# An expert's hidden features formed turned: weights standing in TensorE's array, and a ScalarE copy of each tile's weights

## The chip, the cores and the metric

The kernel runs on one core of a Trainium2 chip. A time is the device time of one execution in microseconds (us). Before the change it was 764.09 us, the median of three runs (763.78 to 767.37). One more execution was profiled: it took 762.74 us, and its span, from the first instruction to the last, is 761.0 us. All rows, durations and starts below are those of this one execution. Engines are named as the profile names them: PE is TensorE's matmul and PEld its weight load, DVE is VectorE, ACT is ScalarE, POOL is GpSimd, SP is SyncE; a name with a q (SPq, ACTq) is that engine's own queue of DMA issues and register work. L1168 is line 1168 of the kernel.

## What is computed

4 x 1024 tokens of 256 features pass through cross-attention (16 heads, a context of 77 rows) with a residual and layer norms, and then through a mixture of 32 experts with a shared expert beside it. Everything is float32. The part that the change touches is the expert:

```python
def swiglu(x, w1, w2, w3):
    return jax.nn.silu(x @ w1) * (x @ w3) @ w2
...
scores = jax.nn.softmax(xf @ Wg, axis=-1)
weights, indices = jax.lax.top_k(scores, 4)
for e in range(32):
    tok, w = ...                      # the tokens that chose expert e, and their gates
    out = swiglu(xf[tok], W1[e], W2[e], W3[e]) * w[:, None]
    y = y.at[tok].add(out)
z = swiglu(xf, Ws1, Ws2, Ws3)         # the shared expert, all tokens
return y + z
```

W1[e] and W3[e] are 256 x 128 and W2[e] is 128 x 256. An expert's tokens are worked in tiles of 128 rows.

## The kernel before

**Stages.** Up to about 400 us the kernel does the attention, 32 tiles of 128 queries, and for each block of 512 tokens the routing: the normalised rows are scattered to DRAM (`xr`), sorted by expert. From 449 us to 720 us it works the experts' tiles; this is the stage of the change. From 721 us to the end it does the shared expert's last three blocks, gathers the experts' results and stores.

**Experts' tiles.** At least 128 tiles are worked in a loop written out in full; after it a `Switch` chooses, by a number found at run time, how many more groups of eight tiles follow (here two, so 144 tiles in all). All experts' weights lie in SBUF in one tile `we`; for each expert there are W1 and W3, cut in two halves of 128 input features (`KC` = 2), and then W2. Which expert a tile belongs to is known only at run time: its number is loaded into a register (`registers`, L1084, a TENSOR_LOAD for eight tiles at a time), and an instruction's address is computed from it.

Four steps make a tile, and the loop runs them as a pipeline: in iteration j, step i is done for tile j - i, so PE's order in an iteration is in(j), mid(j-1), turn(j-2), out(j-3).

- `expert_in` (L1160, L1162): PE turns the tile's 128 gathered rows (two transposes, `pgT`), DVE copies them to `gT`.
- `expert_mid` (L1168, L1176, L1177): PE multiplies with `gT` standing in the array and 256 columns of W1 and W3 moving, for both halves (`peh`: tokens down, features across). ACT applies silu to the first 128 columns, DVE multiplies by the other 128: `h`.
- `expert_turn` (L1182, L1184): PE turns `h` (`phT`), ACT copies it to `ehT`.
- `expert_out` (L1192, L1196, L1197): PE multiplies `ehT` by W2 (`py`), ACT scales by the token's gate into `y`, POOL scatters `y` to DRAM (`ys`) with an indirect DMA.

A float32 matmul shows in the profile as two records, each a weight load and a pass of the moving columns; a transpose shows as one.

**Beside the tiles.** SP fetches the rows of eight tiles at a time (`fetch`, L1106, once in eight iterations, seven ahead), reads back results that are complete (`take`, L1220), and loads blocks of the shared expert's input (`fetch_shared`, L577, into three rotating buffers `sx`; the sixth block on ACT's queue, behind the drained loop). DVE finds each group's places (`find`, L1122 to L1153) and, from tile 88 on, adds the results taken (L1234, L1236). Two blocks of the shared expert (L589, L600, L606, L617, L632) are put between the tiles: block 1 at iterations 3 to 7, block 2 where the loop drains and the Switch ends.

**What sets the order.** Inside `as_written()` every engine runs its instructions in the order in which they are written; nothing is moved by a scheduler. PSUM is one ring of eight banks. Tiles in SBUF have as many buffers as their pool says (`bp`: two, where not stated otherwise), and an instruction that writes a buffer waits for the readers of what was there. Code that follows the Switch waits for each engine's work inside it where it touches the same buffers.

Of the kernel before, what the change touches and what calls it, by code (L numbers as in the profile page):

```python
# [16 lines left out]
P = 128  # L17
NE = 32
# [12 lines left out]
def kernel(  # L31
# [65 lines left out]
    def bank(name):  # L97
        return ps.tile([P, 512], F32, tag="bank", name=name)
# [979 lines left out]
        sends(3)  # L1078
        shared_add(z)
    late_stack.close()  # L1080
    sxp = ctx.enter_context(tc.tile_pool(name="sxp", bufs=3, side="right"))

    def registers(table, j0, engine, most):
        _, vals = nc.values_load_multi_w_load_instructions(  # L1084
            table[0:1, j0 : j0 + RG],
            engines=[engine],
            min_val=0,
            max_val=most,
            skip_runtime_bounds_check_because="whole numbers by their making",
        )  # L1090
        return vals
# [1 line left out]

    bp_stack = ExitStack()
    bp = bp_stack.enter_context(tc.tile_pool(name="bp", bufs=2, reuse_waits="tile"))
    ev, groups = [], {}

    def table(j):
        return (*tabs["a"], j) if j < NA else (*tabs["z"], j - NA)
# [1 line left out]
    def fetch(j):  # L1101

        g = bp.tile([P, RG, ROW], F32, tag="g", name=f"g_{j}")
        r_tab, e_tab, _, _, jt = table(j)
        for i, r in enumerate(registers(r_tab, jt, mybir.EngineType.SP, NE * PLACES)):
            got = nc.sync.dma_start(g[:, i, :], xr[ds(r, P), :])  # L1106
            for x in early if j < NA else scatters:
                tc.add_manual_dep(got.ins, x.name, SYNC, reason="reads what was scattered")
            if j < NA:
                tc.declare_no_dep(got.ins, group="lates", reason="distinct rows")  # L1110
                tc.add_to_no_dep_group("firsts", got.ins)
        ev.extend(registers(e_tab, jt, mybir.EngineType.PE, NE - 1))
        groups[j // RG] = [g]

    def find(j, step):
# [28 lines left out]
        else:  # L1144
# [8 lines left out]
                nc.vector.tensor_tensor(place_, n[3][:, :, 0], far, ALU.add)  # L1153
            n.append(place_)

    def expert_in(j, _):
        g = groups[j // RG][0]
        pt = bank(f"pgT_{j}")
        for k in range(KC):
            nc.tensor.transpose(pt[:, k * P : (k + 1) * P], g[:, j % RG, k * P : (k + 1) * P], ident)  # L1160
        gT = bp.tile([P, KC, P], F32, tag="gT", name=f"gT_{j}")
        nc.vector.tensor_copy(gT.rearrange("p k t -> p (k t)"), pt[:, :D])  # L1162
        return gT

    def expert_mid(j, gT):
        ph = bank(f"peh_{j}")
        for k in range(KC):
            nc.tensor.matmul(  # L1168
                ph[:, : 2 * H],
                gT[:, k, :],  # L1170
                we[:, ds(ev[j] * EW + k * 2 * H, 2 * H)],
                start=(k == 0),
                stop=(k == KC - 1),
            )
        h = bp.tile([P, H], F32, tag="h", name=f"h_{j}")
        nc.scalar.activation(h, ph[:, :H], AF.Silu)  # L1176
        nc.vector.tensor_tensor(h, ph[:, H : 2 * H], h, ALU.mult)  # L1177
        return h

    def expert_turn(j, h):  # L1180
        pt = bank(f"phT_{j}")
        nc.tensor.transpose(pt[:, :P], h, ident)  # L1182
        hT = bp.tile([P, P], F32, tag="ehT", name=f"ehT_{j}")
        nc.scalar.copy(hT, pt[:, :P])  # L1184
        return hT

    def expert_out(j, hT):
        if j in (NE_, NM_) and j not in upto:
            assert len(sents) == j
            upto[j] = list(sents)  # L1190
        py = bank(f"py_{j}")
        nc.tensor.matmul(py[:, :D], hT, we[:, ds(ev[j] * EW + KC * 2 * H, D)], start=True, stop=True)  # L1192
        y = bp.tile([P, D], F32, tag="y", name=f"y_{j}", bufs=6)
        own, place_ = groups[j // RG][3:]
        i = j % RG
        nc.scalar.activation(y, py[:, :D], AF.Identity, scale=own[:, i, 1:2])  # L1196
        sent = nc.gpsimd.indirect_dma_start(  # L1197
            out=ys,
            out_offset=bass.IndirectOffsetOnAxis(ap=place_[:, i : i + 1], axis=0),
            in_=y,  # L1200
            in_offset=None,
        )

        tc.declare_no_dep(sent.ins, group="results", reason="distinct places")
        tc.add_to_no_dep_group("results", sent.ins)
        for j0 in (NE_, NM_):
            if j >= j0:

                tc.declare_no_dep(sent.ins, group=f"takes {j0}", reason="distinct places")
                tc.add_to_no_dep_group(f"results {j0}", sent.ins)  # L1210
        sents.append(sent.ins)
# [34 lines left out]
            out[r0 : r0 + HC * P, :].rearrange("(c p) d -> p c d", p=P), y0[blk][:, c0 : c0 + HC, :]  # L1246
        )

    steps = [expert_in, expert_mid, expert_turn, expert_out]
    made = {}  # L1250
    BL = BM - 1
    adds, adds_l = (
# [2 lines left out]
    with as_written():  # L1255
        fetch(0)
        fetch_shared(1, nc.sync)
        for j in range(NM_ + len(steps)):
            if j % RG == 1 and j + RG - 1 <= NM_:
                fetch(j + RG - 1)  # L1260
            if j in (4 * RG + 4, 5 * RG + 4, 6 * RG + 4):
                fetch_shared(j // RG - 2, nc.sync)
            if j == NE_ + 3:
                for i in range(3):
                    take(i)
            for i, step in enumerate(steps):
                jj = j - i
                if 0 <= jj < NM_:
                    made[jj, i + 1] = step(jj, made.pop((jj, i), None))
            if j in (2, 5, 8, 11):  # L1270
                next(tz)

            for blk, j0 in ((1, 3), (2, NM_)):
                if j == j0:
                    shared_in(blk, 0, AF.Silu)
                    sends(3)
                if j == j0 + 1:
                    shared_mid(blk, 0)
                    shared_in(blk, 1, AF.Silu)
                    sends(3)  # L1280
                if j == j0 + 2:
                    shared_mid(blk, 1)
            if j == 6:
                shared_out(1)
                sends(2)
            assert not left or j < 6
            if j == 7:
                shared_add(1)
            if NE_ + 8 <= j < NM_:
                for i, step in adds[:1]:  # L1290
                    add_taken(i, step, BE * NC)

                    if step == TOPK // 2 and i % HC == 0 and HC <= i <= 2 * NC:
                        store(i // HC - 1, nc.sync)
                del adds[:1]
            if j < NM_ and j % RG in (0, 1, 2):
                find(j // RG * RG, j % RG)
            if j == NM_ - 2 * RG:
                more = {
                    e: nc.values_load(  # L1300
                        tabs["more"],
                        engines=[e],
                        min_val=0,
                        max_val=(NJ - NM_) // RG,
                        skip_runtime_bounds_check_because="at most as many tiles as are laid out",
                    )
                    for e in mybir.ALL_ENGINES
                }
                tc.switch_hint(more, (NJ - NM_) // RG + 1, label="more")
            if j == NM_ + 2:  # L1310
                fetch_shared(5, nc.scalar)
    assert not adds
    ahead = groups[NM_ // RG][0]
    for n in tc.Switch(more, (NJ - NM_) // RG + 1, hint="more"):
        end = NM_ + n * RG
        groups.clear(), made.clear()
        adds = list(adds_l)
        groups[NM_ // RG] = [ahead]
        del ev[NM_ + RG :]
        with as_written():  # L1320
            for i in range(3):
                take(BE * NC + i)
            for j in range(NM_, end + len(steps)):
                if j % RG == 1 and j + RG - 1 < end:
                    fetch(j + RG - 1)
                for i, step in enumerate(steps):
                    jj = j - i
                    if NM_ <= jj < end:
                        made[jj, i + 1] = step(jj, made.pop((jj, i), None))
                if j < end and j % RG in (0, 1, 2):  # L1330
                    find(j // RG * RG, j % RG)
                if j == end:
                    shared_out(2)
                if j == end + 1:
                    shared_add(2)
                if j >= NM_ + 6:
                    for i, step in adds[: 1 + j % 2]:
                        add_taken(i, step, BL * NC)
                    del adds[: 1 + j % 2]
            for i, step in adds:  # L1340
                add_taken(i, step, BL * NC)
# [26 lines left out]
    with as_written():  # L1368
        come = {hb: gather(hb) for hb in (12, 13, 14, 15, 10, 11)}
        shared_in(3, 0, AF.Silu)  # L1370
        shared_in(3, 1, AF.Silu)
        shared_mid(3, 0)
        store(4)
        shared_mid(3, 1)
# [80 lines left out]
```

## Time and profile before

| what | value | where in the profile |
|---|---|---|
| median of three runs | 764.09 us | runs |
| profiled execution, its span | 762.74 us, 761.0 us | runs, page's head |
| granted TensorE clock, mean | 0.989 | cores |
| PE busy, PEld busy | 95%, 71% of the span | page, part 1 |
| DVE, ACT, POOL busy | 63%, 53%, 53% | page, part 1 |
| experts' stage | 449.4 us (first `pgT`) to 720.1 us (last `py`) | tiles pgT, py |
| 450 to 724 us: PE busy | 263.1 of 274 us | windows |
| tiles, records of `pgT`, `peh`, `phT`, `py` on PE | 144; 288, 576, 144, 288 | tiles |

How to read it: "busy" joins the spans of instructions, which overlap on PE, so the cost of a PE instruction is not its duration but the distance from its start to the next one's. A row of groups names line, engine, operation, the tile written and the tiles read, the count, and durations. A row of waits says which engine stood idle at which line until which other line was done.

### The profile page before, as it was taken

The page shows a single profiled execution, that of the slowest core. Times are in us where ns is not written, and L with a number is a line of the kernel's source. Part 1 is how long each engine was busy: PE and PEld are TensorE (multiplying, and loading weights), DVE is VectorE, ACT ScalarE, POOL GpSimd, SP SyncE. Part 2 cuts the span into 40 slices and gives each one's busy share as a digit, 9 for nine tenths or more (in the row PEclk, how much of TensorE's full clock was granted, in tenths as well). Part 3 has the DMA queues.
Part 4 walks back from the last instruction along what each step waited for, and adds up shares of the span by engine and source line. Part 5 has one row for each costly group of instructions (what it writes and reads, how often), then busy time and mean ns, then how long its engine had stood idle before and what let it go on. Part 6 is the DMA issues. An engine that isn't in the chain of part 4 may idle for free. (4 is left out here: it accounts for less than half of the span.)

```text
span 761.0 us, 13078 instructions
## 1 busy us (share of the span) xinstructions
PE 720.0 (95%) x3515; PEld 536.6 (71%) x3515; DVE 478.2 (63%) x1368; ACT 402.3 (53%) x1730; POOL 404.1 (53%) x492
## 2 busy tenths in 40 slices
PE   7999999999999999999987779999999999999996
PEld 5866777677777767777763457788888887876754
DVE  2965565777877878776757433644545466645766
ACT  2658567666777576766553002455555555544310
POOL 1003343346777878777786655565565555553500
PEclk9999999999999999999998989999999999999999
DMA  8930000402217131513136451555746579847594
GB/s 284 342 113 1 1 1 1 132 7 87 100 59 253 47 127 52 170 59 120 74 97 210 140 189 65 159 173 183 224 161 195 166 262 311 258 127 244 186 342 163
DMA packets 78599, 111.98 MB, mean 147 GB/s; under 512 B 8949, under 2 KB 63667, under 8 KB 78515
## 3 DMA queue, kind: packets, MB, share of 16 engines
q1 hardware_dynamic: 60319, 68.76, 29.4%
q0 software_dynamic: 13056, 36.72, 13.0%
q10 hardware_dynamic: 5140, 5.55, 2.1%
q8 instruction: 32, 0.52, 0.3%
q14 instruction: 52, 0.43, 0.2%
HBM read 62.36 MB, written 48.64 MB: 146 GB/s over the span
## 5 line engine op out<-in xcount | busy, mean ns | idle before, releaser
L327 ACT ACTIVATE p<-sc,mx 128x77 f32<-128x77 f32 x512 | 159.5, 352 | 93.2 <-DVE mx L319 93.2
L1197 POOL DMA_INDIRECT ys<-y,place x144 | 138.9, 964 | 124.1 <-ACT y L1196 102.0
L1168 PE MATMUL peh<-we,gT 128*128 x576 | 150.7, 385 | 6.9 <-DVE gT L1162 5.4
L378 PE MATMUL po<-we,pT 128*128 128x256 f32 (+1 forms) x640 | 147.3, 383 | 4.8 <-DVE pT L365 3.4
L555 POOL DMA_INDIRECT xr<-xn,row x128 | 128.1, 1000 | 41.1 <-issue 33.1
L342 POOL TENSOR_TENSOR p<-p,su 128x385 f32<-128x385 f32 (+1 forms) x96 | 91.1, 974 | 97.5 <-DVE su L337 76.5
L311 PE MATMUL sc<-we,qT 128*128 128x385 f32 (+1 forms) x384 | 138.9, 509 | 0.9 <-POOL qT L297 0.9
L378 PEld LDWEIGHTS po<-we,pT 128*128 128x128 f32 (+1 forms) x640 | 118.4, 190 | 27.1 <-DVE pT L365 5.8
L327 ACT ACTIVATION_READ_ACCUMULATOR p<-sc,mx 128x1 f32 x512 | 119.3, 233 | 0.0
L1168 PEld LDWEIGHTS peh<-we,gT 128*128 128x128 f32 x576 | 99.2, 192 | 16.7 <-DVE gT L1162 6.5
L311 PEld LDWEIGHTS sc<-we,qT 128*128 128x128 f32 x384 | 71.1, 189 | 54.3 <-issue 27.7
L1176 ACT ACTIVATE h<-peh 128x128 f32<-128x128 f32 x144 | 40.0, 278 | 116.0 <-PE peh L1168 76.3
L1177 DVE TENSOR_TENSOR h<-peh,h 128x128 f32<-128x128 f32 x144 | 41.9, 291 | 87.1 <-ACT h L1176 80.2
L1192 PE MATMUL py<-we,ehT 128*128 x288 | 86.1, 381 | 0.0
L1196 ACT ACTIVATE y<-py,own 128x256 f32<-128x256 f32 x144 | 68.3, 475 | 17.8 <-PE py L1192 2.0
L319 DVE TENSOR_REDUCE mx<-sc 128x5 f32<-128x385 f32 (+1 forms) x96 | 54.3, 576 | 32.8 <-PE sc L311 30.1
L1162 DVE COPY gT<-pgT 128x256 f32<-128x256 f32 x144 | 60.5, 420 | 19.5 <-PE pgT L1160 9.1
L1160 PE MATMUL pgT<-ident,g 128*128 128x128 f32 x288 | 55.1, 274 | 1.3 <-DMA g<-xr 0.5
L1160 PEld LDWEIGHTS pgT<-ident,g 128*128 128x128 f32 x288 | 40.1, 142 | 17.2 <-issue 2.3
L1192 PEld LDWEIGHTS py<-we,ehT 128*128 128x128 f32 x288 | 43.6, 191 | 11.6 <-issue 0.8
L589 PE MATMUL ph<-sx,ws 128*128 128x512 f32 x96 | 46.0, 628 | 1.6 <-DVE y L1236 1.0
L360 PEld LDWEIGHTS pp<-ident,p 128*128 128x128 f32 x320 | 36.1, 139 | 11.4 <-issue 5.5
(227 smaller groups left out, 927.3 us busy)
## 6 DMA issues: line engine op xcount, KB each, us to landing
g<-xr SPq DMA_DIRECT2D x144, 136.0 KB
gx<-ys SPq DMA_DIRECT2D x20, 512.0 KB
gy<-ys SPq DMA_DIRECT2D x6, 1024.0 KB
xr<-y SPq DMA_DIRECT2D x1, 4352.0 KB
y<-in_x SPq DMA_DIRECT2D x8, 512.0 KB
xnd<-xnT SPq DMA_DIRECT2D x6, 512.0 KB
we<-in_W SPq DMA_DIRECT2D x8, 384.0 KB
out<-y ACTq DMA_DIRECT2D x12, 256.0 KB
```

Source lines behind the costliest of these rows:

```text
L311: nc.tensor.matmul(sc[:, : (h1 - h0) * SK], qTs[blk][:, k, o : o + P], mq[:, b, k, h0 * SK : h1 * SK], start=(k == 0), stop=(k == KC - 1),)
L319: nc.vector.tensor_reduce(mx[:, h0:h1], sv, AX.X, ALU.max, negate=True)
L327: nc.scalar.activation(probs[t][:, h, :], sv[:, h - h0, :], AF.Exp, bias=mx[:, h : h + 1], accum_out=su[:, h : h + 1],)
L342: nc.gpsimd.tensor_tensor(p[:, h0:h1, :], p[:, h0:h1, :], su[:, h0:h1].unsqueeze(2).to_broadcast([P, h1 - h0, SK]), ALU.mult,)
L378: nc.tensor.matmul(po[:, :D], pT[:n, i, :], vo[b][:n, i, :], start=(i == 0), stop=(i == KT - 1))
L555: sct = nc.gpsimd.indirect_dma_start(out=xr, out_offset=bass.IndirectOffsetOnAxis(ap=row[:, i : i + 1], axis=0), in_=xn[:, c, :], in_offse ...
L1160: nc.tensor.transpose(pt[:, k * P : (k + 1) * P], g[:, j % RG, k * P : (k + 1) * P], ident)
L1162: nc.vector.tensor_copy(gT.rearrange("p k t -> p (k t)"), pt[:, :D])
L1168: nc.tensor.matmul(ph[:, : 2 * H], gT[:, k, :], we[:, ds(ev[j] * EW + k * 2 * H, 2 * H)], start=(k == 0), stop=(k == KC - 1),)
L1192: nc.tensor.matmul(py[:, :D], hT, we[:, ds(ev[j] * EW + KC * 2 * H, D)], start=True, stop=True)
L1196: nc.scalar.activation(y, py[:, :D], AF.Identity, scale=own[:, i, 1:2])
L1197: sent = nc.gpsimd.indirect_dma_start(out=ys, out_offset=bass.IndirectOffsetOnAxis(ap=place_[:, i : i + 1], axis=0), in_=y, in_offset=None,)
```

## The change

- `expert_mid` now lets W1's and W3's four blocks of 128 x 128 stand in the array and `gT` (128 columns) move. The features come out down and the tokens across, so silu and product write `ehT` at once. `expert_turn` is gone: no `phT`, no copy of it; in its place stands `expert_rest`, which does nothing.
- Standing weights are read from a fixed address: ACT first copies the tile's 128 x 512 block of `we` to a buffer `w` (`weigh`, two buffers), at an address from its own registers (`eva`, loaded for ACT as `ev` is for PE).
- That copy is a pipeline step of its own, `expert_weigh`, so there are five steps: in(j), weigh(j-1), mid(j-2), rest(j-3), out(j-4). ACT's order in an iteration is w(j-1), silu(j-2), y(j-4).
- Buffers: `gT` three (two before), `ehT` three, `y` five (six), `sx` two (three). For that, the shared expert's fifth block is fetched on ACT's queue at the drained loop's end, and the sixth behind the tiles, after `shared_in(3, 1)`.
- `take` and the first adds are one iteration later.

```diff
-    sxp = ctx.enter_context(tc.tile_pool(name="sxp", bufs=3, side="right"))
+    sxp = ctx.enter_context(tc.tile_pool(name="sxp", bufs=2, side="right"))
...
         ev.extend(registers(e_tab, jt, mybir.EngineType.PE, NE - 1))
+        eva.extend(registers(e_tab, jt, mybir.EngineType.Activation, NE - 1))
...
+    def weigh(j):
+        fixed[j] = bp.tile([P, KC * 2 * H], F32, tag="w", name=f"w_{j}")
+        nc.scalar.copy(fixed[j], we[:, ds(eva[j] * EW, KC * 2 * H)])
...
-        gT = bp.tile([P, KC, P], F32, tag="gT", name=f"gT_{j}")
+        gT = bp.tile([P, KC, P], F32, tag="gT", name=f"gT_{j}", bufs=3)
...
     def expert_mid(j, gT):
+        w = fixed.pop(j)
         ph = bank(f"peh_{j}")
-        for k in range(KC):
-            nc.tensor.matmul(
-                ph[:, : 2 * H],
-                gT[:, k, :],
-                we[:, ds(ev[j] * EW + k * 2 * H, 2 * H)],
...
-        h = bp.tile([P, H], F32, tag="h", name=f"h_{j}")
-        nc.scalar.activation(h, ph[:, :H], AF.Silu)
-        nc.vector.tensor_tensor(h, ph[:, H : 2 * H], h, ALU.mult)
-        return h
-
-    def expert_turn(j, h):
-        pt = bank(f"phT_{j}")
-        nc.tensor.transpose(pt[:, :P], h, ident)
-        hT = bp.tile([P, P], F32, tag="ehT", name=f"ehT_{j}")
-        nc.scalar.copy(hT, pt[:, :P])
+        for f in range(2):
+            for k in range(KC):
+                nc.tensor.matmul(
+                    ph[:, f * P : (f + 1) * P],
+                    w[:, (2 * k + f) * H : (2 * k + f + 1) * H],
+                    gT[:, k, :],
...
+        hT = bp.tile([P, P], F32, tag="ehT", name=f"ehT_{j}", bufs=3)
+        nc.scalar.activation(hT, ph[:, :P], AF.Silu)
+        nc.vector.tensor_tensor(hT, ph[:, P : 2 * P], hT, ALU.mult)
+        return hT
+
+    def expert_weigh(j, gT):
+        weigh(j)
+        return gT
+
+    def expert_rest(j, hT):
         return hT
...
-        y = bp.tile([P, D], F32, tag="y", name=f"y_{j}", bufs=6)
+        y = bp.tile([P, D], F32, tag="y", name=f"y_{j}", bufs=5)
...
-    steps = [expert_in, expert_mid, expert_turn, expert_out]
+    steps = [expert_in, expert_weigh, expert_mid, expert_rest, expert_out]
...
-            if j in (4 * RG + 4, 5 * RG + 4, 6 * RG + 4):
+            if j in (4 * RG + 4, 5 * RG + 4):
                 fetch_shared(j // RG - 2, nc.sync)
-            if j == NE_ + 3:
+            if j == NE_ + 4:
...
-            if NE_ + 8 <= j < NM_:
+            if NE_ + 9 <= j <= NM_:
...
             if j == NM_ + 2:
-                fetch_shared(5, nc.scalar)
+                fetch_shared(4, nc.scalar)
...
         shared_in(3, 1, AF.Silu)
+        fetch_shared(5, nc.scalar)
         shared_mid(3, 0)
```

More of the change, by code (lines that the diff above doesn't have):

```diff
@@ L1095 @@
     bp = bp_stack.enter_context(tc.tile_pool(name="bp", bufs=2, reuse_waits="tile"))
-    ev, groups = [], {}
+    ev, eva, groups = [], [], {}
     def table(j):
@@ L1154, in find @@
             n.append(place_)
+    fixed = {}
+    def weigh(j):
+        fixed[j] = bp.tile([P, KC * 2 * H], F32, tag="w", name=f"w_{j}")
+        nc.scalar.copy(fixed[j], we[:, ds(eva[j] * EW, KC * 2 * H)])
     def expert_in(j, _):
@@ L1165, in expert_mid @@
     def expert_mid(j, gT):
+        w = fixed.pop(j)
         ph = bank(f"peh_{j}")
-        for k in range(KC):
-            nc.tensor.matmul(
-                ph[:, : 2 * H],
-                gT[:, k, :],
-                we[:, ds(ev[j] * EW + k * 2 * H, 2 * H)],
-                start=(k == 0),
-                stop=(k == KC - 1),
-            )
-        h = bp.tile([P, H], F32, tag="h", name=f"h_{j}")
-        nc.scalar.activation(h, ph[:, :H], AF.Silu)
-        nc.vector.tensor_tensor(h, ph[:, H : 2 * H], h, ALU.mult)
-        return h
-    def expert_turn(j, h):
-        pt = bank(f"phT_{j}")
-        nc.tensor.transpose(pt[:, :P], h, ident)
-        hT = bp.tile([P, P], F32, tag="ehT", name=f"ehT_{j}")
-        nc.scalar.copy(hT, pt[:, :P])
+        for f in range(2):
[4 more added lines that the diff above has]
+                    gT[:, k, :],
+                    start=(k == 0),
+                    stop=(k == KC - 1),
+                )
+        hT = bp.tile([P, P], F32, tag="ehT", name=f"ehT_{j}", bufs=3)
[6 more added lines that the diff above has]
+    def expert_rest(j, hT):
         return hT
@@ L1318 @@
         groups[NM_ // RG] = [ahead]
-        del ev[NM_ + RG :]
+        del ev[NM_ + RG :], eva[NM_ + RG :]
         with as_written():
```

## Prediction

> **What bounds the kernel now.** I first read the busy time by stretch, because a share over the whole span mixes stages. In the experts' stage the columns are: stretch, its length, busy time (instructions) of PE, PEld, DVE, ACT, POOL, then granted clock, DMA share, GB/s.
>
> ```profile
> 500.00:560.00 60.00, 60.00 (x334) 50.67 (x333) 28.74 (x95) 33.56 (x111) 35.37 (x38) 1.00 0.61 191
> 560.00:625.00 65.00, 65.00 (x361) 54.98 (x360) 35.53 (x124) 36.31 (x120) 37.93 (x40) 1.00 0.61 199
> 625.00:655.00 30.00, 27.86 (x150) 22.42 (x149) 18.84 (x63) 14.86 (x50) 16.80 (x18) 1.00 0.89 280
> ```
>
> PE is busy for all of 125 us at full clock, and every other engine for about 60% or less. So here a tile costs what PE needs for it. Second, PE's timeline of one tile (start, length, engine, line; x4 joins four records):
>
> ```profile
> 560.53 0.38 PE L1160 MATMUL pgT<-ident,g 128*128 128x128 f32 x2
> 560.75 1.03 PE L1168 MATMUL peh<-we,gT 128*128 x4
> 561.62 0.27 PE L1182 MATMUL phT<-ident,h 128*128 128x128 f32 x1
> 561.73 0.60 PE L1192 MATMUL py<-we,ehT 128*128 x2
> 562.16 0.38 PE L1160 MATMUL pgT<-ident,g 128*128 128x128 f32 x2
> ```
>
> Read the starts: pgT takes 0.22 us, peh 0.87, phT 0.11, py 0.43; the tile's period is 562.16 - 560.53 = 1.63 us. A record of 256 moving columns costs 0.87 / 4 = 0.217, one of 128 costs 0.11. Weight loads lie under the matmul before them. Third, the waits of 470 to 615 us:
>
> ```profile
> DVE h L1177 <- ACT h L1176: 55.1, 80, 0.8
> POOL ys L1197 <- ACT y L1196: 53.2, 75, 2.7
> ACT h L1176 <- PE peh L1168: 34.1, 49, 2.1
> ...
> PE peh L1168 <- DVE eq L1122: 1.1, 1, 1.1
> ```
>
> The others wait, PE hardly ever.
>
> **What goes on PE.** The 144 transposes phT: 0.11 us each, on the path where PE sets the pace.
>
> **What comes on PE.** peh keeps its moving columns, 4 x 256 = 8 x 128, but needs eight weight loads for four, each under a matmul half as long. The nearest row has the same form, float32, 128 x 128 weights, 128 columns, each record with a load of its own: routing's `pf`, four in a row.
>
> ```profile
> 164.76 0.39 PE L519 MATMUL pf<-mask,tri 128*128 128x128 f32 x2
> 164.98 0.39 PE L519 MATMUL pf<-cum,ones 128*128 128x128 f32 x2
> 165.20 0.55 PE L311 MATMUL sc<-we,qT 128*128 128x462 f32 x1
> ```
>
> (165.20 - 164.76) / 4 = 0.11 us per record. So the load (190 ns long in the rows of pf) still hides, and peh becomes 8 x 0.11 = 0.88 us, 0.01 more. With a third decimal the record lies between 0.109 and 0.111, and a tile saves 0.09 to 0.10 us; I take 0.095. New period: 1.535 us. For 144 tiles: **-13.7 us** (-13.0 to -14.4).
>
> A rule that speaks against this stands in the Trainium skill, "TensorE: Matmul & The Clock Gate", Part 3, what overlaps and what doesn't: a weight load is said to overlap a running matmul only when the two use different row groups. All loads here use all rows, so by it load and pass would add up to about 0.22 us per record, peh to 1.76 us, and the kernel would lose some 110 us. In pf, full rows too, records start 0.11 apart, so the row contradicts it and I go by the row.
>
> **ScalarE.** It loses the copy of phT and gains w, 128 x 512 from SBUF. No such copy is in the trace. Bounds: 128 x 512 from PSUM (L434) 586 to 661 ns; SBUF as source adds some 50 ns (L475, 128 x 128 from SBUF, 330, against silu's 278). I take 0.66 us. Today's ACT in one period:
>
> ```profile
> 506.48 0.28 ACT L1176 ACTIVATE h<-peh 128x128 f32<-128x128 f32 x1 [0.61 <-DVE gT L1162]
> 506.66 0.26 ACT L1184 COPY ehT<-phT 128x128 f32<-128x128 f32 x1
> 507.03 0.47 ACT L1196 ACTIVATE y<-py,own 128x256 f32<-128x256 f32 x1
> ```
>
> The sum of lengths goes from 1.01 to 0.28 + 0.47 + 0.66 = 1.41 us, under 1.535. The order matters more. Put zero where an iteration's pgT starts. y starts 0.20 after it (560.73 against 560.53) and ends at 0.67; w runs from 0.67 to 1.33; peh ends near 1.27, silu starts at 1.33; y follows in the next iteration at 1.73. The reader of w is peh one iteration on, with its load at about 1.64. Slack: 0.3 us. Queued behind w are silu and y, and behind silu DVE's product, which now has two iterations until py.
>
> Once in eight tiles ACT also loads its registers, between y's dispatch (0.20) and w. PE's and SP's own loads of this kind (L1084) have medians of 0.53 to 0.82 us, the longest 1.47. With 0.59 and 0.1 for the address, w ends at 1.55 and PE does not wait; with 0.82 it waits 0.14; with 1.47, 0.8. Six loads like the first six (0.8 us together) and a bad one: **+1.2 us**. Bounds: 0, and 18 x 0.31 = 5.6 if each took 0.99.
>
> **More slack for DVE.** gT may be one iteration late, the product too. PE's waits for DVE in the stage after its fill are 1.5 (gT), 1.1 (eq), 1.0 (h) and 0.3 (place), 3.9 us together; most are at places where DVE stands for a DMA (find waits for all of a group's rows). I take **-1.0** (0 to -3.9).
>
> **Where the loop drains.** The results of tiles 126 and 127 now both come after block 2's features; before, 127 alone did. Their scatters take 0.96 us each on POOL, and block 5's fetch (0.35 us on ACT) now stands between the two y. The last scatter is about 0.8 us later against PE. SP's reads wait for it (4.9 us here), and the next group's rows are queued behind them on SP:
>
> ```profile
> SPq L1220 <- DMA ys<-y,place: 8.6, 2, 4.9
> ```
>
> Their landing ended a wait of PE at 704.23, so some 11 tiles' gain (1.0) is not seen there, against more slack for the tiles that wait. **+0.5** (0 to +1.9).
>
> **Behind the last tile.** PE's first work after the Switch waits for DVE's last adds:
>
> ```profile
> 721.00 1.98 PE L589 MATMUL ph<-sx,ws 128*128 128x512 f32 x4 [0.56 <-ACT y L1196]
> 724.00 1.53 PE L589 MATMUL ph<-sx,ws 128*128 128x512 f32 x3 [1.01 <-DVE y L1236]
> ```
>
> The last product now stands behind shared_out's 3.45 us on PE, so DVE's chain of two block adds and eight small ones ends some 0.85 us later; PE may do four more records (1.72 us) before that wait, or none. **+0.5** (-0.9 to +2.5).
>
> **At nothing.** y with five buffers: from y's start (687.32) to the end of SP's wait for its scatter (692.0) are 4.7 us, and five periods are 7.7; uncovered, ACT and all behind it would wait. Block 5's move: 512 KB fetched at about 728, needed near 739.5 (third ph after pz), beside six gathers of 1 MB; at half of that stretch's 256 GB/s it takes 4 us, and PE waits only beyond 11 (bound +2). Fetch 4 has longer. One PSUM bank and two address instructions fewer a tile on PE free what nothing waits for.
>
> **Sum.** -13.7 + 1.2 - 1.0 + 0.5 + 0.5 = -12.5 us, so 762.74 - 12.5 = 750.2 in the profiled execution's own terms. The median of the runs lies 1.35 us above that execution: 764.09 - 12.5 = **751.6 us**.
>
> **Rivals.**
> 1. ScalarE becomes the bound: w is late in each iteration. For it: slack of 0.3 us, and w, silu and y in turn with semaphores and address work between them could make 1.6 us a period. Against: today's rows overlap (copy starts 0.18 after silu, which is 0.28 long). A period of 1.60 saves 0.03 x 144 = 4.3: 759.8 us. 14%.
> 2. Slower: in a row of eight the loads set the pace; pf shows only four. It decides from (0.87 + 0.11) / 8 = 0.122 us per record: above that the tile is slower than today. At 0.13, peh is 1.04 and a tile 0.06 longer, with the other terms +10: about 774 us. For it: load rows of 190 ns against passes of 110. Against: pf. 6%.
> 3. The change takes the transpose from PE but the stage does not end sooner, since DVE's adds set the pace from tile 88 and DMA is at 89% in 625 to 655: about 763 us. Against: DVE's work per tile is 0.42 + 0.29 and one add of 0.50 in the mean (0.68, 0.42, 0.42), 1.21 us; in the Switch, with three adds in two iterations, 1.46; PE's is 1.535. 6%.
> 4. The forecast: 74%, 745 to 757.
>
> **Numbers.** All terms at their good ends give -19.2 (744.9), at their bad ends about -1 (763). The range 745.5 to 760 takes in the forecast and rival 1 and leaves out rivals 2 and 3 and the rarest sums. A measurement of this kernel can tell about 0.5%, 3.8 us, from no change. Faster by more: the forecast and most of rival 1 (below 760.3), 84%; within: the rest of 1 and rival 3, 10%; slower: 6%.
>
> **What would show it.** Right: starts of peh's eight records 0.11 apart, pgT to pgT 1.53 to 1.54 us, PE busy throughout 500 to 625. Wrong: a row PE or PEld peh <- ACT w of more than 5 us (rival 1); records 0.12 or more apart (rival 2); PE waiting for gT or g, with the stage as long as before (rival 3); PE waiting for sx near 735, or the wait after the Switch longer than 3 us (the tail's terms).

## The result and the profile after

The changed kernel took **769.61 us** (median of nine runs, 761.20 to 773.27) against 762.94 us of the kernel before (nine runs beside it, 760.69 to 767.37). The ratio is 1.0056, 95% interval 1.0029 to 1.0083: slower by half a per cent, where 751.6 us was forecast. The profiled execution took 768.18 us with a span of 766.4 us. Two disturbed runs of the changed kernel are left out of the ratio. As the experiments show, this holds where it was measured; on two other chips the same program is 1.1 to 1.2% faster than before.

First the windows of the stretches shown of before (columns as there):

```profile
500.00:560.00 60.00, 57.95 (x435) 52.42 (x434) 27.82 (x94) 43.58 (x110) 34.98 (x37) 1.00 0.57 181
560.00:625.00 65.00, 62.39 (x469) 56.44 (x468) 33.16 (x118) 46.23 (x118) 37.22 (x39) 1.00 0.60 192
625.00:655.00 30.00, 27.82 (x206) 24.65 (x206) 19.61 (x68) 19.70 (x51) 16.81 (x18) 1.00 0.87 274
```

PE, which was busy for all of 500 to 625, now stands idle for 4.7 us of these 125, at full clock. ACT is busy for 72%, so its work does not fill the stretch. PE's timeline of one undisturbed tile:

```profile
520.25 0.38 PE L1168 MATMUL pgT<-ident,g 128*128 128x128 f32 x2
520.47 1.06 PE L1179 MATMUL peh<-gT,w 128*128 128x128 f32 x8
521.37 0.60 PE L1204 MATMUL py<-we,ehT 128*128 x2
521.80 0.38 PE L1168 MATMUL pgT<-ident,g 128*128 128x128 f32 x2
```

From pgT to pgT are 1.55 us, and peh's eight records take 521.37 - 520.47 = 0.90: the tile on PE is nearly as forecast. The waits of 470 to 615 us (total, times, longest) show who stops it:

```profile
ACT ehT L1187 <- PE pgT L1168: 16.9, 12, 2.3
...
PEld peh L1179 <- ACT w L1162: 4.7, 9, 0.9
```

Over the longer stretch of 475 to 690 us, which is compared with other runs below:

```profile
PEld peh L1179 <- ACT w L1162: 8.4, 16, 0.9
...
PE peh L1179 <- ACT w L1162: 4.2, 12, 0.7
```

PE's loads wait for the copy w, and ScalarE's silu (ehT L1187) waits for PE, up to 2.3 us. The second is the odd one: silu needs peh, not the later pgT that the row names. Here are ACT and then PE around one such place:

```profile
522.00 0.47 ACT L1208 ACTIVATE y<-py,own 128x256 f32<-128x256 f32 x1 [0.16 <-issue]
522.37 0.61 ACT L1162 COPY w<-we 128x512 f32 x1
524.13 0.28 ACT L1187 ACTIVATE ehT<-peh 128x128 f32<-128x128 f32 x1 [1.15 <-PE pgT L1168]
524.31 0.47 ACT L1208 ACTIVATE y<-py,own 128x256 f32<-128x256 f32 x1
524.66 0.62 ACT L1162 COPY w<-we 128x512 f32 x1
```

```profile
522.91 0.60 PE L1204 MATMUL py<-we,ehT 128*128 x2
523.35 0.38 PE L1168 MATMUL pgT<-ident,g 128*128 128x128 f32 x2
523.56 1.06 PE L1179 MATMUL peh<-gT,w 128*128 128x128 f32 x8
524.46 0.60 PE L1204 MATMUL py<-we,ehT 128*128 x2
524.89 0.38 PE L1168 MATMUL pgT<-ident,g 128*128 128x128 f32 x2
525.34 0.71 PE L1179 MATMUL peh<-gT,w 128*128 128x128 f32 x4
```

The peh that this silu needs ended at 523.07 by PE's rows (its last record; ends are modelled), and the copy w ahead of silu ended at 522.98. Yet ACT stands until 524.13. It then works without a pause, but the next w starts at 524.66 and ends at 525.28, and PE's peh starts at 525.34 where it would have started at 525.11. The trace also records the changes of the semaphore on which PE signals that it is done. In an undisturbed tile these are 0.2 us or more apart; here three come at 524.11, 524.15 and 524.20, for work of PE that ended at 523.07, 523.51 and 523.73. So PE's signals came up to 1.0 us late, and bunched. I count as a bunch two or more changes less than 60 ns apart. Between 475 and 690 us there are **29** in the changed kernel and **1** before. An undisturbed w ends 0.47 us ahead of its reader, so a signal more than 0.5 us late stops PE.

The place above is one of many alike. From tile 16 to tile 112 a peh starts late in 23 places. In each of them it starts 0.05 us behind the end of its w, and the silu that stands ahead of that w in ScalarE's order had started 0.39 to 2.39 us behind the end of its own peh. These places cost PE 10.1 us ahead of peh's first record and, with the short delays within the eight records, 12.5 us in all. On chip D (below) the same stretch loses 0.8 us.

Behind the last tile:

```profile
720.91 1.55 PE L1204 MATMUL py<-we,ehT 128*128 x6
726.03 2.48 PE L589 MATMUL ph<-sx,ws 128*128 128x512 f32 x4 [3.57 <-DVE gx L1246]
```

Here ph is the shared expert's features and pz its second product. PE does none of the shared expert's records before DVE's last adds (before: four of them), and from 727.3 to 730.7 its clock is half.

How far the changed kernel is behind (+) or ahead (-), in us, at the same points of both profiles; the second row is a pair of profiles on another chip (D, below):

| | tile 0 | tile 16 | tile 112 | tile 143 | last py | first ph behind | its pz | end |
|---|---|---|---|---|---|---|---|---|
| first profiles | +3.0 | -1.3 | +0.8 | +1.1 | +2.0 | +5.0 | +5.5 | +5.4 |
| chip D | +0.1 | -3.7 | -11.4 | -13.8 | -12.9 | -9.9 | -9.6 | -9.6 |

The +3.0 at tile 0 lies ahead of the change: PE begins the shared expert's last 14 records of pz 1.45 us later (447.68 against 446.23), and works on them at half clock from 447.4 to 450.9 us, which makes the rest.

### The profile page after: what moved, and what is told of

Read it like the earlier page. It is cut to its first block, busy times and chain, and to the rows that moved or that the text cites. A ratio compares the mean times of both kernels' runs of the same rounds, so it can differ in the third digit from the quotient of the medians.

```text
span 766.4 us, 13672 instructions
## 1 busy us (share of the span) xinstructions
PE 716.5 (93%) x3947; PEld 549.7 (72%) x3947; DVE 475.2 (62%) x1368; ACT 444.2 (58%) x1730; POOL 404.6 (53%) x492
## 4 chain that ended last, share of the span: by engine, by line
PE 74%; DVE 8%; ACT 8%; issue 5%; POOL 2%; DMA 1%; another core or an unknown queue 1%; ACTq 0%; DVEq 0%; POOLq 0%
PE peh L1179 16%; PE po L378 15%; PE sc L311 13%; PE py L1204 7%; PE ph L589 6%; ACT p L327 5%; PE pgT L1168 5%; PE pz L617 2%; PE pp L360 2%; ACT w L1162 1%; PE pvT L684 1%; POOL xr L555 1%; DVE mx L319 1%; PE pm L708 1%; PE pvo L708 1%
## 5 line engine op out<-in xcount | busy, mean ns | idle before, releaser
L1179 PE MATMUL peh<-gT,w 128*128 128x128 f32 x1152 | 156.3, 279 | 12.2 <-ACT w L1162 5.3
L1179 PEld LDWEIGHTS peh<-gT,w 128*128 128x128 f32 x1152 | 140.9, 192 | 20.3 <-ACT w L1162 9.7
L1188 DVE TENSOR_TENSOR ehT<-peh,ehT 128x128 f32<-128x128 f32 x144 | 41.6, 289 | 97.5 <-ACT ehT L1187 68.3
L1162 ACT COPY w<-we 128x512 f32 x144 | 88.4, 615 | 6.2 <-issue 3.6
L1187 ACT ACTIVATE ehT<-peh 128x128 f32<-128x128 f32 x144 | 40.1, 278 | 70.4 <-PE peh L1179 27.0
```

Source lines behind the costliest of these rows:

```text
L1162: nc.scalar.copy(fixed[j], we[:, ds(eva[j] * EW, KC * 2 * H)])
L1179: nc.tensor.matmul(ph[:, f * P : (f + 1) * P], w[:, (2 * k + f) * H : (2 * k + f + 1) * H], gT[:, k, :], start=(k == 0), stop=(k == KC - 1),)
```

## The experiments

**Theories.** A: the loss is a late w, because PE's signals come late. B: ScalarE's register loads and address work hold it. C: the eight loads set PE's pace. C fell with the timeline above (0.112 us per record). The first four kernels ran on one chip, here A, where the kernel before took 763.7 us. I count the first profiles to it, because the kernel before takes the same time there; that it was the same chip is not on record.

**More slack for w.** The copy of tile j+2 is written ahead of silu of tile j.

```diff
+        if j + 2 < until[0]:
+            weigh(j + 2)
         hT = bp.tile([P, P], F32, tag="ehT", name=f"ehT_{j}", bufs=3)
         nc.scalar.activation(hT, ph[:, :P], AF.Silu)
```

> The changed kernel, with ScalarE's copy of tile j+2 written ahead of silu of tile j, not behind y: it can start as soon as peh of tile j has ended, and by the changed kernel's rows its slack to its reader rises from 0.47 us to 1.3 us at most. Theory A (the loss is a late w: PE's completion signals come up to 1.3 us late and bunched, ScalarE waits for them, and 0.47 us of slack do not cover that): PE's waits for w in 500 to 625 us fall from 7.9 us to below 2, the tiles come at 1.55 us each, and the time is 768 - 11 = 757 us, give or take 4. Rival B (ScalarE's register loads and its address work hold it): the lateness of silu comes before w's successor as often as now, some of it is covered, 761 to 766. Rival C (the eight loads set PE's pace): no change, 768.

Measured: 776.13 us, 1.0164 (1.0135 to 1.0194). 60 bunches, and PE waits more for w, not less; the waits of 475 to 690 us:

```profile
ACT w L1162 <- PE pgT L1168: 51.4, 29, 3.7
...
PEld peh L1179 <- ACT w L1162: 20.3, 24, 2.1
...
ACT w L1162 <- PE peh L1179: 17.9, 19, 2.1
PE peh L1179 <- ACT w L1162: 13.8, 16, 1.9
```

Here w itself waits for PE's signal of the peh whose buffer it overwrites (where that is late, the row names pgT, as above). In 35 of 45 places where ScalarE stood idle ahead of it, w starts over 0.4 us behind the end of that peh, up to 3.4 us. A cure by slack was wrong on this chip; so was my figure of at most 1.3 us for the lateness.

**Addresses fixed in the program.** The weights copied are then not those of the tile's expert; the amount of work is the same.

```diff
-        nc.scalar.copy(fixed[j], we[:, ds(eva[j] * EW, KC * 2 * H)])
+        nc.scalar.copy(fixed[j], we[:, (j % NE) * EW : (j % NE) * EW + KC * 2 * H])
```

> The changed kernel, but each copy w reads an address fixed in the program (the weights of expert j mod 32, so not those of the tile's expert), so ScalarE has no register load and no address instruction in the tiles. Theory A (PE's signals are late, whatever ScalarE does): the same bursts, PE still waits some 5 to 8 us for w in 500 to 625, the time within 3 us of 768. Rival B (ScalarE is held by its register work): the bursts are gone, PE does not wait for w, 755 to 758 us.

770.46 us, 1.0076 (1.0047 to 1.0106), 37 bunches, and PE still waits for w: 6.3 us (PEld) and 3.5 us (PE) in 500 to 625, where the changed kernel waits 5.2 and 2.7. Theory B is out.

**The copy on DVE.** `nc.vector.tensor_copy` in place of `nc.scalar.copy`, registers on DVE.

> The changed kernel, but DVE makes the copy w, its register loads with it; ScalarE is left with silu and y. DVE's sum per tile goes from 0.71 to about 1.2 us, with find and adds some 1.5 in the worst stretches. Theory A: late signals from PE now hold gT and the product as well as w on DVE, so PE still waits, for w or gT, by 5 us or more in 500 to 625; time 763 to 780. Rival B (it is ScalarE's own doing): PE's waits for w go, and the time is 756 to 760 up to the adds from tile 88 on.

777.75 us, 1.0172 (1.0135 to 1.0209), but only 4 bunches. Six or seven tiles of eight come at 1.55 us up to tile 88; the loss there is at the turn of a group, with periods such as 2.18 and 1.71 us, where DVE has the group's places to find beside the copy. That this work of DVE is the cause was not tested by itself. DVE copies faster (0.43 us against 0.62), and is the wrong engine here all the same. Theory A as stated (5 us or more of waits in any case) did not foresee the few bunches.

**The old features, the copy kept.** peh, silu, product and phT as before the change; w is made and not read.

> The changed kernel with the features formed as before (gT standing, W1 and W3 moving from the address in PE's register, the transpose phT and its copy back), while ScalarE still copies w for every tile, which nothing reads. Theory A has the bunched signals come from PE's new sequence with its eight loads: here they are as rare as before the change (one in the tiles), and silu is late only where ScalarE itself is full; 763 to 768 us. Rival B (the copy and its register work hold ScalarE): silu is late by 0.5 to 1.3 us in most tiles here too, whether or not PE waits for it.

771.71 us, 1.0101 (1.0067 to 1.0136). 5 bunches, tiles at 1.63 us, tiles 16 to 112 in 158.6 us against 158.8 before: in the tiles ScalarE's copy costs nothing by itself. The time is lost elsewhere, against the first profile of the kernel before: 3.1 us by tile 16 (tile 0 starts 10.3 us late, at 459.6 us, with 10 us of half clock from 447.8 on, and most of that is made up), 5.0 us from tile 127 to 128, and 3.1 us behind the last tile, where PE stands 3.7 us.

What went with many bunches on chip A was the absence of something: in the kernel before, the old features and the copy on DVE, one PE instruction per tile waits for PE's own signal; in the others none does. That is theory S. The next four kernels were to test it.

**out ahead of in.** The steps of an iteration are written in the order weigh, mid, rest, out, in.

```diff
-            for i, step in enumerate(steps):
+            for i, step in [(i, steps[i]) for i in [1, 2, 3, 4, 0]]:
```

> The changed kernel with the steps of an iteration written in the order weigh, mid, rest, out, in. On PE the cyclic order stays peh, py, pgT; DVE copies gT behind the product in place of ahead of it, so gT has one tile less of slack. By this order py no longer needs a wait for DVE; what is left on it is a wait for PE's own signal of an earlier matmul. Theory S (formed from the rows so far): the kernels in whose tiles one PE instruction waits for PE's own signals (before the change, the old features with the copy, the copy on DVE) show next to no bunched signals, those without such a wait (the changed kernel, fixed addresses, the copy ahead of silu) show 25 to 130. By it the bunches go here, the tiles come at 1.55 us, PE waits below 2 us for w in 500 to 625, and the time is 756 us, give or take 4. Rival W (bunches come where PE's loads wait for ScalarE's copy): as the changed kernel, 765 to 772.

**in between mid and out** (`[1, 2, 0, 3, 4]`).

> The changed kernel with the steps written in the order weigh, mid, in, rest, out: PE goes peh, pgT, py, and py has no wait at all, neither for DVE nor for PE's own signal. Theory S: bunched signals as in the changed kernel (20 or more in 500 to 690), 764 to 772 us. If theory S is wrong and the order of DVE's copies is what matters, it goes the way of the kernel with out ahead of in.

**Without the empty step.** `steps = [expert_in, expert_weigh, expert_mid, expert_out]`, the reads of results and the adds one iteration earlier.

> The changed kernel without its empty step between mid and out (a pipeline of four steps as before): py comes one tile earlier, and PE's features wait for ScalarE only, so that PE needs no separate wait instruction in a tile. Theory S: PE has no wait for its own signals here, the bunches stay, and a late silu now also reaches py by DVE's product: 766 to 776 us. Rival E (the separate wait instruction on PE is what holds the signals): no bunches, 756 to 760.

**Standing weights from a fixed place.**

```diff
-        w = fixed.pop(j)
+        fixed.pop(j)
+        w = we[:, (j % NE) * EW : (j % NE) * EW + KC * 2 * H]
```

> The changed kernel, but peh reads its standing weights from a fixed place in the experts' weights (those of expert j mod 32, not the tile's); ScalarE still makes every copy w, and nothing reads it. PE keeps its eight loads and never waits for w. Theory S: there is no wait for PE's own signals, so the bunches stay and silu is late by up to 1.3 us, but only y and the product can stop PE: the time falls to 757 to 763. Rival W: no bunches, and 755 to 758.

These four ran on another chip, B, where the kernel before takes 746.93 us. out ahead of in: 734.74, 0.9837 (0.9816 to 0.9859). in between: 741.74, 0.9930 (0.9903 to 0.9957). Without the empty step: 741.56, 0.9921 (0.9906 to 0.9936). Fixed weights: 738.54, 0.9879 (0.9862 to 0.9896). None has a single bunch, those without a wait for PE's own signal included. So nothing was learned on S; the question became whether the chip makes the bunches.

**The changed kernel on other chips.** Chip C:

> The changed kernel itself, on the chip of this call. The last four kernels ran on a chip where the kernel before took 747 us (granted clock 0.996) and not 763 (0.988), and none of them showed a bunched signal. Theory S (a wait for PE's own signal keeps them in time) says nothing of chips: 25 or more bunches in 500 to 690 here, whatever the chip, and a ratio to the kernel before of 1.00 to 1.01. Theory K (the bunches belong to the chip or its condition on which the changed kernel was first profiled): on a chip with a kernel before of 747 us there are none, tiles come at 1.55 us, and the ratio is 0.985 to 0.992.

> The order weigh, mid, rest, out, in once more, beside the changed kernel on one chip. Theory S: no bunches on any chip, ratio to the kernel before 0.981 to 0.988. Theory K: on a chip where the changed kernel shows bunches, this one shows them too, and its ratio is about 1.00 there; elsewhere 0.984.

> The pipeline of four steps once more, beside the other two. It has no wait for PE's own signal in a tile. Theory S: bunches wherever the changed kernel shows them. Rival E (the separate wait instruction on PE holds the signals): none even where the changed kernel shows them. Theory K: bunches exactly on a chip where the changed kernel shows them.

The changed kernel: 739.30 us, **0.9888** (0.9865 to 0.9911), no bunch. out ahead of in: 733.71, 0.9822 (0.9809 to 0.9836). Without the empty step: 741.84, 0.9934 (0.9920 to 0.9949). Chip D, with the kernel before profiled as well:

> The kernel before the change, for its profile on the chip of this call. If the chip is of the kind with 747 us: tiles at 1.63 us as in the first profile (theory K gives the tiles no part in the difference), and the 16 us lie outside them, most of them in stretches of half clock between 400 and 460 us.

> The changed kernel. Theory K: 1.00 to 1.01 of the kernel before with 25 or more bunches on a chip where that takes about 763 us, 0.985 to 0.992 with none where it takes about 747. In both, PE stands 4 to 5 us between the last py and the shared expert's features, and a stretch of half clock begins there.

> Order weigh, mid, rest, out, in. On a chip of the 763 us kind, theory S (its wait for PE's own signal): no bunches, 0.98 to 0.99; theory K alone: 20 or more, 0.995 to 1.01. On the other kind: 0.98 to 0.985, and PE's gap behind the last py below 2 us with no half clock right after it.

The kernel before: 748.11 us in its one run (746.82 in the median of seven beside it), no bunch. The changed kernel: 738.52, **0.9883** (0.9865 to 0.9901). out ahead of in: 734.13, 0.9832 (0.9814 to 0.9850). Theory K, that the bunches belong to the chip or its condition, holds: the same program has 29 bunches in the first profile and none on C and D. As only one such chip was met, and only early in the series, the chip and its condition at the time cannot be told apart. On chip D the changed kernel's windows and, for 475 to 690 us, PE's wait for w are:

```profile
475.00:600.00 125.00, 125.00 (x973) 116.87 (x972) 67.16 (x230) 101.60 (x243) 76.50 (x81) 1.00 0.63 203
```

```profile
PEld peh L1179 <- ACT w L1162: 1.6, 2, 0.8
...
PE peh L1179 <- ACT w L1162: 1.1, 2, 0.6
```

PE is busy throughout, as was forecast.

The kernel before also differs between the chips, 763 against 747 us, and not as I expected, by half clock alone. Up to 395 us the two profiles of it agree within 0.6 us; by 468 us the first is 14.9 us behind, and at the end 14.6. 10.2 us more at half clock explain 5.1 of them. In the same stretch SP's queue issues the first rows. First the kernel before in the first profile, then on chip D (start, length, instructions):

```profile
428.26 9.40 SPq L1106 DMA_DIRECT2D g<-xr  x7
```

```profile
427.64 4.67 SPq L1106 DMA_DIRECT2D g<-xr  x8
```

An issue takes 1.34 us in the one and 0.58 in the other; register moves of SP between them take up to 702 ns, against 29. So on that chip not only PE's signals come late. What the traces record of PE's signals, and how often silu starts over 0.4 us behind the end of its peh when ScalarE stood idle ahead of it:

| kernel, chip | signals recorded, of PE's signalling instructions | bunches, 475 to 690 us | late silu, 475 to 690 us | a PE wait for its own signal in each tile |
|---|---|---|---|---|
| before, first profile | 842 of 1245 | 1 | 1 of 122 | yes |
| changed, first profile | 898 of 1099 | 29 | 32 of 87 | no |
| copy ahead of silu, A | 934 of 1099 | 60 | silu stands behind w | no |
| fixed addresses, A | 934 of 1099 | 37 | 38 of 88 | no |
| copy on DVE, A | 858 of 1100 | 4 | 4 of 121 | yes |
| old features, A | 848 of 1245 | 5 | 3 of 101 | yes |
| all fourteen profiles on B, C and D | all or nearly (1083 of 1099 at the least) | 0 | 0 | both |

The bunches alone would be a weak count, since a bunch shows only where both of its changes are recorded, and the kernels with few bunches have the fewest on record (in 475 to 690 us 202 of 506 before, 272 of 375 in the changed kernel). The late silu needs no such record and says the same. With the copy on DVE, though, 15 of 68 gT copies start over 0.4 us behind their pgT (3 of 58 before), so the signals there are better but not in time. ScalarE's and DVE's signals are missing on that chip too (661 of 826 and 929 of 1210 recorded, first profile before). Whether the recording itself holds the signals up there, no run settles.

**The order in the Switch alone.** The edit of out ahead of in, made only in the Switch's loop, on chip D.

> The changed kernel with the order weigh, mid, rest, out, in inside the Switch alone, so only for the last 16 tiles. Theory T (the wait behind the last tile comes with the order of the last steps, and the half clock with the wait): PE's gap before the shared expert's features falls from 4 to 5 us to about 1, no half clock begins there, and the kernel is 3 to 6 us faster than the changed kernel beside it. Rival: the half clock comes by its own timing, then only the 3 us of the wait go.

737.74 us, 0.9873 (0.9853 to 0.9893): the same as the changed kernel. PE still stands 4.0 us behind the last tile and half clock begins there. Theory T, that the order of the last steps makes the wait, fell. With the same order in both loops the wait is 0.59 us in all four profiles of out ahead of in, so the order in the loop ahead of the Switch has a part in it.

**Two places further in the PSUM ring** (chip D again).

```diff
                 fetch_shared(4, nc.scalar)
+                for i in range(2):
+                    nc.tensor.transpose(bank(f"pad_{i}")[:, :P], ident, ident)
```

> The changed kernel with two transposes of the identity (0.2 us of PE, their results unread) into two banks of the PSUM ring after the drained loop, so that all banks of the Switch and behind it are two places further in the ring. Theory R (the wait behind the last tile is set by which bank of the ring falls to the first features, and by who read it last): the first features start within 1.5 us of the last py's end, PE's later records wait for DVE at most 2 us, and the kernel is 2 to 6 us faster than the changed kernel's 0.9885 of before. Rival (any order stands until DVE's last adds): a gap of 3.9 to 5.1 us as in the changed kernel, same time.

733.70 us, **0.9832** (0.9812 to 0.9851), 4.8 us below the changed kernel's earlier runs on this chip. PE behind the last tile, and the window after:

```profile
691.65 1.98 PE L589 MATMUL ph<-sx,ws 128*128 128x512 f32 x4 [0.61 <-ACT y L1208]
694.01 6.25 PE L589 MATMUL ph<-sx,ws 128*128 128x512 f32 x14 [0.37 <-DVE y L1248]
```

```profile
695.00:710.00 15.00, 15.00 (x45) 8.13 (x44) 9.04 (x13) 1.79 (x3) 0.00 (x0) 1.00 0.88 332
```

The same places of the changed kernel on that chip:

```profile
696.46 4.03 PE L589 MATMUL ph<-sx,ws 128*128 128x512 f32 x5 [3.50 <-DVE gx L1246]
```

```profile
695.00:710.00 15.00, 13.54 (x32) 6.66 (x33) 6.71 (x11) 1.79 (x3) 1.24 (x2) 0.89 0.73 279
```

As theory R, that the bank on which the first features fall sets the wait, had it: with nothing changed but two transposes that take two banks, the wait went from 3.50 to 0.61 and 0.37 us, and the clock from 0.89 to 1.00. Which reader the bank waits for I did not trace, and other shifts of the ring were not run. The count of banks in a tile is not all of it, since out ahead of in takes as many as the changed kernel and does not wait.

**The copy ahead of silu, and out ahead of in, once more** (chip D).

> The copy w of tile j+2 ahead of silu of tile j, once more. Theory K (late signals belong to one chip): on a chip where the kernel before takes about 747 us no bunches, tiles at 1.55 us, and a ratio of 0.985 to 0.992, like the changed kernel: what it does to w's slack is then worth nothing. If the order itself is bad, 1.00 or more here too. On a chip of the 763 us kind: 1.01 to 1.02 as before.

> Order weigh, mid, rest, out, in. On a chip of the 763 us kind: theory S no bunches and 0.98 to 0.99, theory K 20 or more and 0.995 to 1.01. On the other kind once more 0.980 to 0.985 with no bunches; a fourth chip would show how far that ratio holds.

The copy ahead of silu: 735.18, 0.9855 (0.9830 to 0.9880), no bunch and no late w; the 1.0164 belonged to chip A. It is a little under the changed kernel because PE stands 2.4 us, not 3.5, behind the last tile and keeps its clock. out ahead of in: 734.68, 0.9843 (0.9818 to 0.9869).

## Why the prediction was wrong, by its own steps

**What comes on PE** (-13.7). The mechanism was right: phT is gone and the loads hide. Had loads of 0.19 us and passes of 0.11 added up, a record would have taken 0.30 us (the prediction put 0.22). It takes 0.1117 us, not 0.11, so a tile saves 1.628 - 1.546 = 0.082 us and 144 tiles 11.8. On chip D tiles 16 to 112 took 149.2 us against 157.0: 7.8 of 96 x 0.082 = 7.9 are there.

**ScalarE** (+1.2). This is the step that failed in the measured result, at "peh ends near 1.27, silu starts at 1.33". The price of w (0.62 for 0.66) and the slack (0.47 for 0.3) were near enough, and the register loads harmless. But silu starts when PE's signal comes, and on this chip it came 0.39 to 2.39 us later in the 23 places that stopped PE. Tiles 16 to 112 took 160.9 us, 1.676 each: 96 x (1.676 - 1.546) = 12.5 us lost, where the term had 1.2 for the whole stage and these tiles' gain is 7.9. Before, ScalarE had no copy that PE waited for one tile later, and its silu was late there once in 122. I had taken rival 1 for a question of ScalarE's sum of work; w did come late, by the cause of a signal. Which property of PE's new sequence makes the signals late there stays open: theory S fits the six profiles that it was read from, and no kernel that tests it met such a chip again.

**More slack for DVE** (-1.0). On chip D the first 16 tiles gain 3.8, of which 1.3 are the period: -2.5. Between 439 and 480 us PE's wait for gT falls from 1.8 to 0.2 us there; the rest of the gain I did not trace.

**Where the loop drains** (+0.5). From tile 127 to 128: 10.88 became 11.92, and on chip D 11.21 became 12.26: +1.05, inside the bounds.

**Behind the last tile** (+0.5, to +2.5). Wrong on every chip: from the last py to pz, +3.4 in the first profiles and +3.3 on D. The text said that PE does "four more records (1.72 us) before that wait, or none"; it was none. The change takes one bank fewer in a tile, which I had costed at nothing ("free what nothing waits for"): by the experiment with two more banks, it most likely moved what follows in the ring, so that the first features fell on a bank that comes free only with DVE's last adds (the row's releaser). And behind a wait that long PE works at half clock, which I had not in the sum. The pause from the last py to the first features, and the half clock that begins within 2 us of its end, in all twenty profiles:

| pause, us | profiles | with half clock |
|---|---|---|
| 0.56 to 0.62 | 7 | 0 |
| 2.44 | 2 | 1 |
| 3.50 to 4.49 | 11 | 11 |

Each half clock lasts 3.4 or 6.8 us, so costs PE up to 1.7 or 3.4, less where it begins within the pause. In each of the twenty profiles the starts of half clock lie whole multiples of 3.41 us apart, so it is decided at fixed points in time, and where a pause falls matters. The 2.44 us on chip A (730.54 to 732.98) lie between two such points, 730.3 and 733.8, and half clock follows; on chip D (691.44 to 693.87) the point 693.3 divides them, and none follows. The Trainium skill, "TensorE: Matmul & The Clock Gate", Part 1, the HAM clock gate, says that the clock halves after at least one idle window of about 3.4 us, and that the window runs freely. The second part agrees with the multiples; the first does not hold to the letter, as in the first profile of the changed kernel PE had worked for 1.3 of the 3.4 us ahead of the half clock at 727.3.

**Sum.** The changed kernel's 738.52 against 746.82 on chip D are -8.3 us. With the pause taken out by the ring, that chip gives 733.70 - 746.97 = -13.3 us, where -12.5 was forecast. So the sum of the tiles' terms holds on a chip without late signals, in part by luck: the term of PE was 1.9 too large (11.8 for 13.7) and that of DVE's slack 1.5 too small. The tail's term was mis-sized by 3. The rest is the chip: the two pairs of profiles end 15.0 us apart (+5.4 and -9.6), of which 2.9 lie ahead of tile 0 and 12.0 between tiles 0 and 143; that turned the sign.

## What to carry to other kernels

A pipeline step that feeds PE from another engine lives on the latency of PE's signals, so look for when the signal came and not only for when the work ended. More slack is no sure cure: the copy ahead of silu made the loss larger on chip A, and on chip D there was little to win (148.4 us against 149.2 for tiles 16 to 112). Profile a second chip before explaining a loss by the order of the work. When a change alters how many banks of a ring a tile takes, look at what follows the loop, and try the ring a few places further. Count a pause of PE of 3.5 us or more twice: for itself, and for up to 1.7 or 3.4 us lost to half clock behind it.

## What the runs showed of the hardware

Chips can differ by 2% on the same program: 763 us, and 747 us on the three others, nearly all of it (14.3 of 14.6 us in profiles of the kernel before) in the stretch of 395 to 468 us. On the first SP's register moves took up to 702 ns in place of 29, and in the changed kernel PE's signals came up to 2.4 us late; why is open. A float32 record of 128 columns with a full load of its own (192 ns) starts every 0.1117 us in rows of eight. A 128 x 512 float32 copy within SBUF takes 0.43 us on DVE and 0.61 to 0.62 on ScalarE.
